# Grouping the small matrix products of a windowed-attention kernel by pairs of steps

## The chip, the cores and the metric

The kernel runs on one core of a Trainium2 chip. The metric is the device time of one launch, in microseconds (us). Three runs of the kernel before gave 4153.67, 4155.52 and 4155.97 us; the median is 4155.52 us.

## What is computed

Eight images `x` of 256 channels and 64 x 64 pixels go through two layers, each of which adds to its input. Both normalise over groups of 8 channels first (`_gn`).

Layer 0 makes a 3 x 3 filter for every pixel from two hidden maps and applies it to a third map:

```python
x1 = _conv1x1(x, w1, b1); x2 = _conv1x1(x, w2, b2); x3 = _conv1x1(x, w3, b3)
h = jnp.concatenate([x1, x2u], axis=1)            # x2u: 3 x 3 neighbours of x2
h = jax.nn.relu(_bn(h, ...)); h = _conv1x1(h, cw1)
h = jax.nn.relu(_bn(h, ...)); w = _conv1x1(h, cw2, cb2)
out = jnp.einsum('bgskhw,bgkhw->bgshw', x3u, w)   # 9 taps per pixel
```

Layer 1 adds an attention over 7 x 7 neighbours with 4 heads to a depthwise convolution whose nine results are weighted by a softmax:

```python
att = jax.nn.softmax(jnp.einsum('bdn,bdkn->bnk', q, uk + upe[None]), axis=-1)
out_att = jnp.einsum('bnk,bdkn->bdn', att, uv)
wts = jax.nn.softmax(jnp.einsum('oc,bchw->bohw', Wfc, x)..., axis=2)
hid = jax.nn.relu(_dwconv(xr, w1)); oc = _dwconv(hid, w2)
out_conv = jnp.sum(oc * wts, axis=1)
return rate1 * out_att + rate2 * out_conv
```

All is computed in fp32.

## The kernel before

An image is cut into 8 bands of 8 rows. Layer 1 takes the 64 bands in turn (`g` from 0 to 63). A band has 8 steps, s0 to s7: two channel halves `ct` by four column pairs `m`. Layer 0 of a later band runs inside the same steps (its maps 12 bands ahead, its hidden maps 11, its taps 10), so that layer 0 ends after about band 52. Before band 0 layer 0 runs alone.

The order on every engine is written out by hand. In `conv_layers_kernel` each step calls its parts in turn. `advance()` moves a clock by one, six times a step, and `after(n, f)` puts a piece of work n such places later. Each engine works through its instructions in that order.

A step does this:

- `scores` makes the attention scores of two 8 x 8 pixel tiles (L703, 64 x 64 parts of the array), and `weighted_values` (L747, 64 columns of the array) multiplies older probabilities with the values. Both write the tile `sco`, of two PSUM banks, of which there is one. DVE adds the mask and takes the maximum (L712), and `add_values` (L757) adds the weighted values to the output rows `xr`.
- `exponentials` (L720) and `probabilities` (DVE reciprocal L727, ACT scaling L729) finish the softmax. `transposed` (L735) turns the probabilities of the step before; ACT copies them (L737).
- `branch_weights` (L825) makes two of the nine weight maps of the dynamic convolution by 128 x 512 products, and ACT takes their exponential into `ex` (L830), of which there are three buffers. POOL adds them up (L1026).
- The depthwise convolutions are taps on DVE (L782, L808), four a step. Queries, keys, values and their transposes come at fixed steps (L637, L658, L563, L607).

At the end of a channel half `dynamic_sum` closes the weights: POOL makes the total (L838), DVE adds one and takes the reciprocal of the first half (L845, L846), then of the second half (L850), and POOL multiplies twice and adds to `xr` (L855, L856, L857). For `ct` 1 this falls into s0 to s2 of the next band, for `ct` 0 into s4 to s6.

Layer 0 inside the steps: `small_maps` (L328) in s0 with ACT's copies (L343, L347), `value_maps` (L369), `hidden_maps` (L418, L429) in two parts, and `tap_weights` (L447) in s1, s3 and s5, three taps each. Each tap is one DVE product (L460, two `prod` buffers) and one POOL addition to `xg` (L468). For the three taps of a call, DVE's products come 1, 2 and 7 (or 5) places later.

[...]two for `sco`, one for `acc` and five that the tag `gen` hands round.

Of the kernel before, what the change touches and what calls it, by code (L numbers as in the profile page):

```python
# [39 lines left out]
TG = 3  # L40
# [25 lines left out]
TAPS_AT = (1, 3, 5), (0, 2, 4)  # L66
PRODUCTS_AT = ((1, 2, 7), (1, 2, 5), (1, 2, 7)), ((7, 14, 10), (9, 17, 13), (12, 20, 16))
# [19 lines left out]
def conv_layers_kernel(ctx: ExitStack, tc: tile.TileContext, ins: dict, out: bass.AP):  # L87
# [98 lines left out]
    def layer1_loads():  # L186


        last = w1.tile([P, NCT, 1, C], F32, tag="rec", name="last", bufs=1)
        for f in late:  # L190
            f()
        nc.scalar.dma_start(out=last, in_=wfc_in[:, :, KK - 1 :])

        def first():
            nc.vector.tensor_scalar(wv, wv, rate1, None, ALU.mult)

        def difference(kt):
            nc.vector.tensor_sub(wfc[:, kt], wfc[:, kt], last[:, kt].to_broadcast([P, KK - 1, C]))  # L200

        return [first, lambda: difference(0), lambda: difference(1)]
# [22 lines left out]
    def gn_affine(sts, means, name, done):  # L225


        n = len(sts)
        mv = stat.tile([P, n, 2], F32, name=f"mv_{name}", tag=f"mv{n}")
        for ct, st in enumerate(sts):  # L230
            nc.vector.bn_aggr(mv[:, ct, :], st)
        mean, var = mv[:, :, 0], mv[:, :, 1]
        gm, d, sc, bi = (stat.tile([P, n], F32, name=f"{v}_{name}", tag=f"{v}{n}") for v in ("gm", "d", "sc", "bi"))

        def group_means(v, k):
            pg = ps.tile([P, n], F32, name=f"pg_{name}_{k}", tag="gen", bufs=5)
            nc.tensor.matmul(pg, means, v, start=True, stop=True)
            return pg


        def a1():
            pg = group_means(mean, 0)
            after(2, lambda: a2(pg))

        def a2(pg):
            nc.vector.tensor_copy(gm, pg)
            for ct in range(n):
                c = slice(ct, ct + 1)
                nc.vector.tensor_scalar(d[:, c], pg[:, c], mean[:, c], None, ALU.subtract)
                nc.vector.tensor_scalar(d[:, c], d[:, c], d[:, c], var[:, c], ALU.mult, ALU.add)  # L250
            after(5, a3)

        def a3():
            pg = group_means(d, 1)
            after(2, lambda: a4(pg))

        def a4(pg):
            nc.vector.tensor_scalar(sc, pg, GN_EPS, None, ALU.add)
            after(2, a5)

        def a5():
            nc.scalar.activation(sc, sc, AF.Sqrt)
            after(4, a6)

        def a6():
            nc.vector.reciprocal(sc, sc)
            for ct in range(n):
                c = slice(ct, ct + 1)
                nc.vector.tensor_scalar(bi[:, c], gm[:, c], sc[:, c], -1.0, ALU.mult, ALU.mult)
            done(sc, bi)  # L270

        after(3, a1)
# [15 lines left out]
    def scaled_weights(b):  # L288
# [11 lines left out]
        def through(bi):  # L300
            pb = ps.tile([P, 1 + NCT], F32, tag="gen", name=f"pb_{b}", bufs=5)
            for m, to, w in ((0, 0, w12), (0, 64, w12), (1, 0, w3[:, :, :P]), (2, 0, w3[:, :, P:])):
                for kt in range(NCT):
                    nc.tensor.matmul(
                        pb[to : to + w.shape[2], m : m + 1], w[:, kt], bi[:, kt : kt + 1],
                        start=(kt == 0), stop=(kt == NCT - 1),
                    )
            after(2, lambda: biases(pb))
# [11 lines left out]
    def small_maps(b, i):  # L320


        im = images[b]

        p12 = ps.tile([P, R // 2, W], F32, tag="gen", name=f"p12_{b}_{i}", bufs=5)
        for kt in range(NCT):
            for u in range(2):
                nc.tensor.matmul(  # L328
                    p12[64 * u : 64 * u + 64], im.w12s[:, kt, :],
                    im.xc[i][:, kt, u * BAND // 2 : (u + 1) * BAND // 2],  # L330
                    start=(kt == 0), stop=(kt == NCT - 1),
                )
        return lambda: write_maps(b, i, p12)
# [28 lines left out]
    def value_maps(b, i, mt):  # L362
# [4 lines left out]
        p3 = ps.tile([P, BAND], F32, tag="gen", name=f"p3_{b}_{i}_{mt}", bufs=5)  # L367
# [41 lines left out]
    def hidden_maps(b, i, at):  # L409
# [5 lines left out]
        def hidden(t):  # L415
            n = P if t == 0 else 96
            hid = w0.tile([P, R, W], F32, tag="hid", name=f"hid_{b}_{i}_{t}", bufs=2)
            nc.scalar.activation(  # L418
                hid[:n], im.x2[i][:n, t : t + R, :], AF.Relu, bias=bn1b[:n, t : t + 1], scale=bn1s[:n, t : t + 1]
            )  # L420
            hids.append(hid)

        def conv(first, last):
            if first == 0:
                im.ph = ps.tile([P, SR, W], F32, tag="gen", name=f"ph_{b}_{i}", bufs=5)
            for t in range(first, last):
                n = P if t == 0 else 96
                for q in range(NQR):
                    nc.tensor.matmul(  # L429
                        im.ph[q * REL : (q + 1) * REL], c1[:n, t], hids[t][:n, q * SR : (q + 1) * SR],  # L430
                        start=(t == 0), stop=(t == 2),
                    )

        def relu():
            nc.scalar.activation(h2n[i % 2][:, :, :W], im.ph, AF.Relu, bias=bn2b, scale=bn2s)

        hidden(0)
        for n, f in zip(at, (lambda: hidden(1), lambda: conv(0, 2), lambda: hidden(2), lambda: conv(2, 3), relu)):
            after(n, f)

    def tap_weights(b, i, u, alone, at):
# [3 lines left out]
        pw = ps.tile([P, TG, SR * HP], F32, tag="gen", name=f"pw_{b}_{i}_{u}", bufs=5)  # L445
        for j in range(TG):
            nc.tensor.matmul(  # L447
                pw[:, j], c2[:, TG * u + j], h2n[i % 2].rearrange("p r c -> p (r c)"), start=True, stop=True
            )

        def product(j):
            k = TG * u + j
            if alone and j == TG - 1:
# [11 lines left out]
            if alone and j == TG - 1:  # L465
# [11 lines left out]
        def gather(prod):  # L477
            if u == 0:
                im.part = score_tile(f"sum_{b}_{i}").rearrange("p t (s r c) -> p t s r c", r=SR, c=W)
            for t in range(2):  # L480
                nc.tensor.matmul(
                    im.part[:, t], ident, rows(prod)[:, t * SHARE // 2 : (t + 1) * SHARE // 2],
                    start=(u == 0), stop=(u == KK // TG - 1),
# [18 lines left out]
        for j, n in enumerate(at):  # L502
            after(n, lambda j=j: product(j))


    def norm_rows(b):
# [9 lines left out]
        def by_channel(both):  # L516
            pg = ps.tile([P, NCT, 2], F32, tag="gen", name=f"pgc_{b}", bufs=5)
# [33 lines left out]
    def values(b, j, ct):  # L551
# [3 lines left out]
        pv = ps.tile([P, R, W], F32, tag="gen", name=f"pv_{b}_{j}_{ct}", bufs=5)  # L555
# [45 lines left out]
    def value_tile(b, j, u):  # L601
        im = images[b]
        n = min(R, WP - j * R) * KW
        pvt = ps.tile([CHUNK, 2, C], F32, tag="gen", name=f"pvt_{b}_{j}_{u}", bufs=5)
# [22 lines left out]
    def queries(b, i, ct):  # L627
# [7 lines left out]
        pq = ps.tile([P, R, W], F32, tag="gen", name=f"pq_{nm}", bufs=5)  # L635
# [10 lines left out]
    def keys(b, i, ct):  # L646
# [7 lines left out]
        for a in range(first, last, R):  # L654
            n = min(R, last - a)
            pk = ps.tile([P, R, W], F32, tag="gen", name=f"pk_{b}_{i}_{ct}_{a}", bufs=5)
# [37 lines left out]
    def scores(b, i, ct, m, sco):  # L694
# [4 lines left out]
        nm = f"{b}_{i}_{ct}_{m}"  # L699
        for t in range(2):  # L700
            for h in range(2):
                c0 = (2 * m + t) * TQ
                nc.tensor.matmul(  # L703
                    sco[half[t], h, :NKEY], qb[half[h], 2 * m + t].rearrange("p r c -> p (r c)"),
                    kb[half[h], :, c0 : c0 + KW], start=True, stop=True,
                )

# [3 lines left out]
        for h in range(2):  # L711
            nc.vector.tensor_tensor_reduce(  # L712
                prob[:, h, :NKEY], sco[:, h, :NKEY], mask, -1.0, 3.0e38, ALU.add, ALU.min, nmax[:, h : h + 1]
# [17 lines left out]
    def transposed(nm, prob):  # L731
        ptp = ps.tile([CHUNK, 2, 2, P], F32, tag="gen", name=f"ptp_{nm}", bufs=5)
# [7 lines left out]
    def weighted_values(b, i, ct, m, pt, sco):  # L740
        im = images[b]
        po = sco[:, 0, 256 : 256 + 2 * NQ].rearrange("p (r c) -> p r c", r=R)
# [10 lines left out]
        return po  # L753

# [66 lines left out]
    def branch_weights(b, i, ct, m, j, ex):  # L821

        pf = ps.tile([P, R, W], F32, tag="gen", name=f"pf_{b}_{i}_{ct}_{m}_{j}", bufs=5)
# [8 lines left out]
    def dynamic_sum(b, i, ct, ex, oc):  # L832
# [6 lines left out]
        rec = w1.tile([P, BAND], F32, tag="rec", name=f"rec_{b}_{i}_{ct}", bufs=1)  # L839
# [29 lines left out]
    def beside(g, s):  # L869
# [52 lines left out]
        if 0 <= g + AHEAD < B * NB:  # L922
            bq_, iq = divmod(g + AHEAD, NB)
            if alone and s == 0:
                mid.append(lambda: small_maps(bq_, iq)())
# [4 lines left out]
        if 0 <= g + AHEAD - 1 < B * NB and s == (2 if alone else 1):  # L930
            at = (3, 7, 8, 12, 16) if alone else (5, 13, 14, 19, 21)
            end.append(lambda: hidden_maps(*divmod(g + AHEAD - 1, NB), at))
        if 0 <= g + AHEAD - 2 < B * NB and s in TAPS_AT[alone]:
            u = TAPS_AT[alone].index(s)
# [28 lines left out]
    with tc.manual_schedule():  # L963
# [20 lines left out]
        pending, before, conv = [], None, None  # L984
        for g in range(-AHEAD, B * NB):
            b, i = divmod(g, NB)
            for s in range(STEPS):
# [3 lines left out]
                if g >= 0:  # L991
                    if s == 0 and g + AHEAD < B * NB:
                        mid.append(small_maps(*divmod(g + AHEAD, NB)))
                    nm = f"{b}_{i}_{ct}_{m}"
                    sco = score_tile(nm)
                    weighted = [(a, weighted_values(*a, pt, sco)) for a, pt in pending]
                    prob, nmax = scores(b, i, ct, m, sco)
                    for a, po in weighted:
                        add_values(*a, po)
                    pending = [] if before is None else [(before[:-1], transposed(nm, before[-1]))]  # L1000
                    tot = exponentials(nm, prob, nmax)
                advance()
                if g >= 0:
                    ex, exb = w1.tile([P, 2, BAND], F32, tag="ex", name=f"ex_{nm}", bufs=3), ex if m else None
                    branch_weights(b, i, ct, m, 0, ex)
                    if m in (0, 2):
# [33 lines left out]
        for last in (before, None):  # L1040
            sco = score_tile(f"end{last is None}")
            weighted = [(a, weighted_values(*a, pt, sco)) for a, pt in pending]
            for a, po in weighted:
# [86 lines left out]
```

## Time and profile before

| | |
|---|---|
| median of three runs | 4155.52 us |
| profiled execution | 4152.64 us |
| its span | 4150.9 us |
| PE busy | 4022.6 us, 97% |
| DVE busy | 3591.9 us, 87% |
| ACT busy | 3081.0 us, 74% |
| POOL busy | 2923.0 us, 70% |
| granted TensorE clock | 0.993 |
| first scores of band 0 | 246.3 us |
| most bands with layer 0 beside them | 61.6 us |
| bands 57 to 61, without layer 0 | 53.1 us |

A busy share is an average over the whole span. Matmuls are pipelined and their ends are modelled, so PE's start times say more than its busy time. A band's time is read from one band's first score matmul to the next one's.

### The profile page before, as it was taken

Reading aid. Unit: us, or ns where it says so; the run is one execution under the profiler, and the core shown is the slowest. Engines: PE = TensorE matmul, PEld = TensorE weight load, DVE = VectorE, ACT = ScalarE, POOL = GpSimd, SP = SyncE. Lnnn points to the kernel's source line nnn. Section 1 sums busy time; section 2 is a strip of 40 time slices with the busy share of each in tenths; the row PEclk is TensorE's granted clock in tenths of the full one; section 3 lists DMA queues with packets and bytes.
Section 4 is the critical chain, followed back from the end, with each engine's and each line's share of the span. In section 5 each row is a group of like instructions: output and inputs, shape, how many; then the busy total and the mean of one; then the engine's idle time right before and its main releaser. Section 6 shows DMA issues by size and latency. Waiting matters only on the chain.

```text
span 4150.9 us, 72735 instructions
## 1 busy us (share of the span) xinstructions
PE 4022.6 (97%) x25292; PEld 2126.8 (51%) x25292; DVE 3591.9 (87%) x7248; ACT 3081.0 (74%) x7726; POOL 2923.0 (70%) x1902
## 2 busy tenths in 40 slices
PE   6789999999999999999999999999999999999998
PEld 3345555555555555555555555555555555455554
DVE  5878998899898898889998898888988889977777
ACT  3467778777787777877778777777778777687776
POOL 4767777677786777777777777777777677744554
PEclk8999999999999999999999999999999999999999
DMA  8854234234244233334234234244233233111100
GB/s 226 194 135 111 73 91 109 72 94 109 62 101 107 76 94 98 81 94 109 72 85 118 72 94 105 66 101 106 71 82 99 65 87 85 33 41 39 39 28 21
DMA packets 381264, 367.89 MB, mean 89 GB/s; under 512 B 55648, under 2 KB 282720, under 8 KB 380640
## 3 DMA queue, kind: packets, MB, share of 16 engines
q1 hardware_dynamic: 377568, 358.68, 34.3%
q8 instruction: 200, 3.28, 0.3%
q10 hardware_dynamic: 3328, 4.55, 0.3%
q14 instruction: 168, 1.38, 0.1%
HBM read 261.42 MB, written 101.71 MB: 87 GB/s over the span
## 4 chain that ended last, share of the span: by engine, by line
PE 71%; DVE 14%; POOL 6%; ACT 5%; DMA 2%; issue 2%; SPq 1%; POOLq 0%; ACTq 0%; DVEq 0%
PE pf L825 33%; PE ptp L735 5%; PE sco L747 5%; PE pk L658 5%; PE sco L703 5%; PE p L369 5%; DVE prod L460 4%; PE pq L637 4%; POOL xg L468 3%; PE pvt L607 2%; PE pv L563 2%; DVE acc L808 2%; PE pw L447 2%; DVE acc L782 2%; POOL ex L1026 2%
## 5 line engine op out<-in xcount | busy, mean ns | idle before, releaser
L825 PE MATMUL pf<-yp,c_wfc 128*128 128x512 f32 x4096 | 1930.5, 595 | 10.6 <-ACT vc L581 5.0
L468 POOL TENSOR_TENSOR xg<-xg,prod 128x1024 f32<-128x1024 f32 x549 | 1203.9, 2193 | 96.6 <-DVE prod L460 64.1
L825 PEld LDWEIGHTS pf<-yp,c_wfc 128*128 128x128 f32 x4096 | 729.9, 190 | 690.5 <-issue 619.4
L1026 POOL TENSOR_TENSOR ex<-ex,ex 128x1024 f32<-128x1024 f32 x384 | 907.7, 2364 | 61.9 <-ACT ex L830 57.2
L830 ACT ACTIVATE ex<-pf 128x512 f32<-128x512 f32 x1024 | 607.3, 593 | 297.9 <-POOL ex L1026 141.3
L782 DVE SCALAR_TENSOR_TENSOR acc<-yp,c_chan,acc 128x504 f32<-128x504 f32 (+3 forms) x1104 | 766.2, 694 | 42.3 <-ACT acc L773 21.7
L460 DVE SCALAR_TENSOR_TENSOR prod<-pw,c_par,x3q 128x1040 f32<-128x1040 f32 x576 | 733.9, 1281 | 66.8 <-PE pw L447 21.6
L808 DVE SCALAR_TENSOR_TENSOR acc<-hid,c_chan,acc 128x504 f32<-128x504 f32 (+3 forms) x1024 | 757.8, 740 | 20.2 <-ACT acc L802 2.1
L855 POOL TENSOR_TENSOR ex<-ex,rec 128x512 f32<-128x512 f32 x127 | 162.3, 1278 | 809.5 <-DVE rec L850 767.1
L729 ACT ACTIVATE prob<-prob,tot 128x196 f32<-128x196 f32 x1024 | 411.6, 450 | 387.2 <-DVE tot L727 386.4
L712 DVE CUSTOM_DVE_ANT_0 prob<-sco,c_mask 128x196 f32<-128x196 f32 x1024 | 325.5, 355 | 272.4 <-PE sco L703 272.0
L720 ACT ACTIVATE prob<-prob,nmax 128x196 f32<-128x196 f32 x1024 | 461.4, 454 | 46.9 <-DVE nmax L712 45.3
L747 PEld LDWEIGHTS sco<-pt,vt 112*64 112x64 f32 x8160 | 283.8, 137 | 182.3 <-issue 51.7
L737 ACT COPY pt<-ptp 112x512 f32<-112x512 f32 x511 | 297.0, 581 | 105.0 <-PE ptp L735 103.0
L735 PE MATMUL ptp<-ident,prob 128*112 128x128 f32 x2044 | 341.7, 287 | 31.2 <-ACT prob L729 30.5
L747 PE MATMUL sco<-pt,vt 112*64 112x64 f32 x8160 | 347.0, 227 | 0.0
L735 PEld LDWEIGHTS ptp<-ident,prob 128*112 128x112 f32 x2044 | 203.9, 133 | 201.4 <-issue 77.7
L703 PE MATMUL sco<-kb,qb 64*64 64x196 f32 x4096 | 295.2, 357 | 0.0
L563 PE MATMUL pv<-yp,c_wv 128*128 128x512 f32 (+2 forms) x576 | 247.3, 554 | 0.6
L369 PE MATMUL p<-xc,w3s 128*128 128x512 f32 x512 | 244.4, 601 | 0.0
L658 PE MATMUL pk<-yp,c_wk 128*128 128x512 f32 (+2 forms) x576 | 240.8, 545 | 0.0
L637 PE MATMUL pq<-yp,c_wq 128*128 128x512 f32 x512 | 240.6, 592 | 0.0
(140 smaller groups left out, 5294.0 us busy)
## 6 DMA issues: line engine op xcount, KB each, us to landing
x<-x3n SPq DMA_DIRECT2D x128, 264.0 KB, 2.1
x3q<-x SPq DMA_DIRECT2D x128, 264.0 KB, 7.2
xc<-in_x SPq DMA_DIRECT2D x64, 512.0 KB, 5.0
xg<-in_x SPq DMA_DIRECT2D x256, 128.0 KB, 4.8
x<-xg SPq DMA_DIRECT2D x256, 128.0 KB, 2.4
yp<-x SPq DMA_DIRECT2D x128, 256.0 KB, 3.3
xr<-x SPq DMA_DIRECT2D x64, 512.0 KB, 5.8
out_x<-xr SPq DMA_DIRECT2D x64, 512.0 KB, 3.1
```

The source lines that it names most:

```text
L369: nc.tensor.matmul(p3, im.w3s[:, kt, mt * P : (mt + 1) * P], im.xc[i][:, kt, :], start=(kt == 0), stop=(kt == NCT - 1),)
L460: nc.vector.scalar_tensor_tensor(prod[:, :, :RUN], pw[:, j, :RUN].unsqueeze(1).to_broadcast([P, SHARE, RUN]), par[:, PCB2 + k : PCB2 + k + 1],
L468: nc.gpsimd.tensor_add(im.xg[i], im.xg[i], rows(prod))
L703: nc.tensor.matmul(sco[half[t], h, :NKEY], qb[half[h], 2 * m + t].rearrange("p r c -> p (r c)"), kb[half[h], :, c0 : c0 + KW], start=True, ...
L720: nc.scalar.activation(prob[:, h, :NKEY], prob[:, h, :NKEY], AF.Exp, bias=nmax[:, h : h + 1], scale=-1.0, accum_out=tot[:, h : h + 1],)
L735: nc.tensor.transpose(ptp[:, h, ch], prob[:, h, ch * CHUNK : (ch + 1) * CHUNK], ident)
L747: nc.tensor.matmul(po[half[h], :, t * TQ : (t + 1) * TQ], im.vt[i + ch, m][:n, t, (2 * ct + h) * HD : (2 * ct + h + 1) * HD], pt[:n, h, ch ...
L782: nc.vector.scalar_tensor_tensor(o, yp[:, ct, ra + dr : rb + dr, ca + dc : cb + dc], chan[:, ct, CW1 + k : CW1 + k + 1], o, ALU.mult, ALU.add,
L808: nc.vector.scalar_tensor_tensor(o, hid[:, ra + dr : rb + dr, ca + dc : cb + dc], chan[:, ct, CW2 + k : CW2 + k + 1], o, ALU.mult, ALU.add,)
L825: nc.tensor.matmul(pf, wfc[:, kt, 2 * m + j, ct * P : (ct + 1) * P], images[b].yp[i][:, kt, PAD : PAD + R], start=(kt == 0), stop=(kt == N ...
L830: nc.scalar.activation(ex[:, j].rearrange("p (r c) -> p r c", r=R), pf, AF.Exp)
L1026: after(4, lambda ex=ex, exb=exb: nc.gpsimd.tensor_add(ex, ex, exb))
```

## The change

Even steps now do the small products for two steps. One `sco` tile takes the scores of both, side by side. A new tile, `small`, of one bank, takes the weighted values of two older steps, and, in s0, the small maps, and in s6 the hidden convolution, which is now done in one piece. `gen` has four banks. The mask and maximum stay one step at a time (`masked`). The odd steps' transposes stand after the first weight map instead of among the small products. Weighted values of s7 and s3 are added to `xr` in s2 and s6, where they were added in s1 and s5.

Taps are made two at a time in s1 to s5 (the last call has one); both products come at the first two places after. The buffer `rec` is gone (the reciprocal is written into `ex`), and `hid` has three buffers.

```diff
-TG = 3
+TG = 2, 3
...
-TAPS_AT = (1, 3, 5), (0, 2, 4)
-PRODUCTS_AT = ((1, 2, 7), (1, 2, 5), (1, 2, 7)), ((7, 14, 10), (9, 17, 13), (12, 20, 16))
+TAPS_AT = (1, 2, 3, 4, 5), (0, 2, 4)
+PRODUCTS_AT = ((1, 2),) * 5, ((7, 14, 10), (9, 17, 13), (12, 20, 16))
...
-        p12 = ps.tile([P, R // 2, W], F32, tag="gen", name=f"p12_{b}_{i}", bufs=5)
+        p12 = home[:, 2 * P :].rearrange("p (r c) -> p r c", r=R // 2)
...
-        def conv(first, last):
-            if first == 0:
-                im.ph = ps.tile([P, SR, W], F32, tag="gen", name=f"ph_{b}_{i}", bufs=5)
-            for t in range(first, last):
+        def conv(home):
+            ph = home[:, 2 * P : 3 * P].rearrange("p (r c) -> p r c", r=SR)
+            for t in range(3):
...
+    def score_of(sco, h, m):
+        return sco[:, h, m % 2 * NKEY : (m % 2 + 1) * NKEY]
...
+    def small_tile(nm):
+
+        return ps.tile([P, 4 * P], F32, tag="small", name=f"small_{nm}")
+
+    def weigh_steps(steps, home):
+
+        po = home[:, : 2 * P].rearrange("p (s r c) -> p s r c", s=2, r=R)
+        return [(a, weighted_values(*a, pt, po)) for a, pt in steps]
...
-        rec = w1.tile([P, BAND], F32, tag="rec", name=f"rec_{b}_{i}_{ct}", bufs=1)
+        rec = ex[:, 0]
...
-                    if s == 0 and g + AHEAD < B * NB:
-                        mid.append(small_maps(*divmod(g + AHEAD, NB)))
                     nm = f"{b}_{i}_{ct}_{m}"
-                    sco = score_tile(nm)
-                    weighted = [(a, weighted_values(*a, pt, sco)) for a, pt in pending]
-                    prob, nmax = scores(b, i, ct, m, sco)
+                    weighted = []
+                    if m % 2 == 0:
+                        sco = score_tile(nm)
+                        for e in range(2):
+                            scores(b, i, ct, m + e, sco)
+                        small = small_tile(nm)
+                        weighted, pending = weigh_steps(pending, small), []
+                        if s == 0 and g + AHEAD < B * NB:
+                            mid.append(small_maps(*divmod(g + AHEAD, NB), small))
+                        if s == 6 and convs:
+                            convs.pop()(small)
+                        if before is not None:
+                            pending.append((before[:-1], transposed(nm, before[-1])))
+                    prob, nmax = masked(nm, m, sco)
                     for a, po in weighted:
                         add_values(*a, po)
-                    pending = [] if before is None else [(before[:-1], transposed(nm, before[-1]))]
                     tot = exponentials(nm, prob, nmax)
                 advance()
                 if g >= 0:
...
                     branch_weights(b, i, ct, m, 0, ex)
+                    if m % 2:
+                        pending.append((before[:-1], transposed(nm, before[-1])))
```

## The prediction

> **What bounds the kernel now.** I read the page's busy shares first, then the start times of PE in one ordinary band (band 12, 1003.35 to 1064.93 us), then the timelines of POOL, DVE and ACT in it, since a busy PE need not be what sets the pace.
>
> ```profile
> PE 4022.6 (97%) x25292; PEld 2126.8 (51%) x25292; DVE 3591.9 (87%) x7248; ACT 3081.0 (74%) x7726; POOL 2923.0 (70%) x1902
> ```
>
> PE looks like the bound. Its timeline around step s5 (start, duration):
>
> ```profile
> 1038.00 1.88 PE L825 MATMUL pf<-yp,c_wfc 128*128 128x512 f32 x4
> 1039.81 0.42 PE L429 MATMUL ph<-hid,c_c 96*32 96x128 f32 x8
> 1040.17 0.69 PE L747 MATMUL sco<-pt,vt 112*64 112x64 f32 x16
> 1040.78 0.57 PE L703 MATMUL sco<-kb,qb 64*64 64x196 f32 x8
> 1041.28 0.65 PE L735 MATMUL ptp<-ident,prob 128*112 128x128 f32 x4
> 1041.77 1.88 PE L825 MATMUL pf<-yp,c_wfc 128*128 128x512 f32 x4
> 1043.49 1.88 PE L563 MATMUL pv<-yp,c_wv 128*128 128x512 f32 x4
> ```
>
> Starts are what counts: a 512-wide product holds PE for 1.72 us before another of its kind, and 1.81 us before a product on part of the array, so that entering costs 0.09 us. Weighted values, scores and transposes then take 0.61, 0.50 and 0.49 us. Adding up the undisturbed start-to-start times of a whole ordinary band gives 60.4 us. It takes 61.6, so 1.2 us are stalls, and they lie in s6 and s7. The other engines say why. POOL, then DVE, then ACT:
>
> ```profile
> 1019.00 1.28 POOL L855 TENSOR_TENSOR ex<-ex,rec 128x512 f32<-128x512 f32 x1 [6.12 <-DVE rec L850]
> 1020.36 1.27 POOL L856 TENSOR_TENSOR oc<-oc,ex 128x512 f32<-128x512 f32 x1
> 1021.71 1.28 POOL L857 TENSOR_TENSOR xr<-xr,oc 128x512 f32<-128x512 f32 x1
> 1022.94 4.46 POOL L468 TENSOR_TENSOR xg<-xg,prod 128x1024 f32<-128x1024 f32 x2
> ...
> 1034.62 4.45 POOL L468 TENSOR_TENSOR xg<-xg,prod 128x1024 f32<-128x1024 f32 x2
> 1039.03 2.37 POOL L1026 TENSOR_TENSOR ex<-ex,ex 128x1024 f32<-128x1024 f32 x1
> 1041.47 1.27 POOL L838 TENSOR_TENSOR ex<-ex 128x512 f32<-128x512 f32 x1
> 1042.70 2.17 POOL L468 TENSOR_TENSOR xg<-xg,prod 128x1024 f32<-128x1024 f32 x1
> ```
>
> ```profile
> 1042.78 2.38 DVE L845 TENSOR_SCALAR ex<-ex 128x512 f32<-128x512 f32 x1 [0.43 <-POOL ex L838]
> 1045.19 1.75 DVE L846 RECIPROCAL rec<-ex 128x256 f32<-128x256 f32 x1
> 1046.86 1.45 DVE L782 SCALAR_TENSOR_TENSOR acc<-yp,c_chan,acc 128x504 f32<-128x504 f32 x2
> ...
> 1049.79 1.75 DVE L850 RECIPROCAL rec<-ex 128x256 f32<-128x256 f32 x1
> ```
>
> ```profile
> 1048.41 0.81 ACT L729 ACTIVATE prob<-prob,tot 128x196 f32<-128x196 f32 x2 [3.71 <-DVE tot L727]
> ```
>
> From the end of L850 at 1018.92 POOL never rests until the total L838 ends at 1042.74, 23.8 us later. DVE waits for it, and L850 of the other channel half ends at 1051.54, 8.8 us on. I call these 32.6 us **half A**. ACT's scaling of the probabilities waited 3.71 us behind it, and PE's transposes behind that. From there DVE, ACT and PE lead back to the next L850 (1080.50): 29.0 us, **half B**. A and B close a loop of 61.6 us through all four engines. POOL's part of half A is 23.3 to 23.9 us in seven of an image's eight bands, and still 23.8 in bands 51 to 53, where PE has less to do. So PE's work is 1.2 us short of the bound, and a saving on PE is worth only what this loop passes on.
>
> [...]the 0.09 us above, 0.10 us more at L747 to L703 (152 ns between starts against 52), 0.06 us at L703 to L735, and some 0.05 us twice for a first weight load that nothing covers. [...]L845 takes 0.42 us (median) with POOL idle and 2.38 us above, where POOL's addition had just begun. [...]I let the mask of an even step wait for the scores of both steps; the trace of before has no such pair.
>
> **The change part by part.**
>
> *PE.* Per pair of steps before: 2 x (0.09 + 0.61 + 0.50 + 0.49) = 3.38 us. After, scores of two steps take [...]0.96 us; weighted values [...]1.09; even transposes 0.49; odd ones, now among full products, 0.44 (what L607 takes); entry 0.09: 3.07 us. The order scores, then weighted values, isn't in the trace; by its other switches the saving is 0.25 to 0.40, I take 0.31. Four pairs: 1.25 us. The hidden convolution in one piece, about 0.80 us against 0.58 + 0.36: 0.14 us. So PE's band falls from 60.4 to 59.0 us, and from 53.1 to 51.9 where layer 0 is over.
>
> *Tap weights in twos.* PE, DVE and POOL do the same nine; each bank is held for less, which pays for the fifth `gen` bank, as do the maps moved to `small`. But the order moves. POOL's queue before L838 held five additions since L850; products now come two in each of s2 to s5, so it holds six: +2.15 us. L845 then meets the next addition as before (2.38 us). And between DVE's first and second half reciprocal now stands a product: +1.21. Half A: 32.6 + 2.15 + 1.21 = 36.0 us. DVE gets there earlier: the wait described next 4.16, six more products 7.3, three masks 1.7, two pairs of additions 1.1, three steps of taps 9.0, keys 1.1, together 24.3 us. So POOL is the limit. ACT's exponentials also wait for these POOL additions through the three `ex` buffers, as before.
>
> *Weighted values a step later.* Those of s3 and s7 are added to `xr` by DVE in s6 and s2, now behind POOL's addition L857 to the same rows, a wait that no L757 has in the kernel before. POOL ends it 4.16 us after DVE starts past L850 (three operations, 1019.00 to 1022.99). DVE has a product (1.12) and the mask (0.56) before it, so it stands 2.4 us; queued behind it are the taps and the reciprocal that ACT's scaling waits for, then PE's odd transposes.
>
> *Half B*, on DVE alone: up to the end of that wait 4.16 us (a product and the mask of s6 lie in it), three more masks 1.7, two pairs of additions to `xr` 1.06, taps and small reciprocals of four steps 11.9, statistics 1.19 + 1.18, keys 1.11, L845 and L846 2.12, L850 1.66: 26.1 us. That is the floor. On the way that sets it before: the reciprocal of s6 comes at 6.2 us; ACT's scaling and the query copy, in its queue, end at 7.7, when PE's transposes get their bank; transposes, three big products and the values' transposes end at 12.2; then PE's group of s0 (scores 0.96, weighted values 1.09, small maps 0.87, transposes 0.49) ends at 15.7; ACT's copy and exponentials 17.2; weight exponential and scaling 18.9; a copy, eight map copies of 0.48, two more and the exponentials of s1 at 25.3; DVE's reciprocal, taps and L850: 28.5. I take 28.3.
>
> *The odd mask* no longer waits for PE (272.0 us in all before, mostly DVE idle that cost nothing). `rec` in `ex` and the third `hid` cost nothing: `ex` is held until L856 anyway.
>
> *Sum.* Loop 36.0 + 28.3 = 64.3 us against 61.6: +2.7. The first band of an image (68.8 us) has 3.2 us of POOL slack in its half A, where I take +1; mean +2.5. Layer 0 runs beside 53 bands: +133 us. Eleven bands without it, bound by PE, gain 1.2 each: -13. The 246 us before band 0 keep three taps a call: 0, within 5. Together +120 on the profiled execution's 4152.6 (span 4150.9 and 1.7 around it): 4273. That execution lies 2.9 under the median of the runs, so 4275.
>
> **The rivals.**
>
> *PE sets the pace and gets its saving.* For it: 97% busy. Against: half A doesn't move with PE's load. It needs one thing: that DVE doesn't stand at `xr`. Without those 2.4 us half B's floor is 23.7 and the loop can be 59.7; it decides once B is under 25.6 (61.6 - 36.0). Then bands take 59.7 to 60.4: 53 x -1.2 to -1.9, and -13: 4040 to 4080; 4000 if every stall goes.
>
> *DVE's floor.* ACT and PE keep up, B is 26.1, the loop 62.1: +0.5 x 53 - 13 = +14, 4170.
>
> *The banks.* Four `gen` banks, with ACT behind in s0 and s1 (7.84 us busy of 7.97 in s1): a further 0.7 us a band, 4310.
>
> *The switch isn't cheaper:* [...]PE at 60.4; the loop hides it, but the last bands lose their gain: 4288.
>
> **How the numbers follow.** Loop as summed, with banks and switch cases, 4220 to 4320: 0.56. DVE's floor and between, 4165 to 4220: 0.21. Faster: 0.18. Within 0.2% (8 us, about what a measurement of this kernel can't tell from none): 0.05. The range 4150 to 4320 leaves out the faster cases and a little above. Half B's bounds, 26.1 and 29.0 as before, give 4160 and 4312.
>
> **What would show it.** Right: POOL's way from the second half reciprocal to the total 26.0 us, half A 36; DVE's first addition to `xr` in s2 and s6 waiting for POOL, some 2 us each; ordinary bands 63 to 65 us, the last ones 52; PE's share down to about 94%. Wrong: half A under 34, or no such wait and bands under 61 us.

## The result, and the profile after

The changed kernel takes 4320.47 us (median of four runs, 4320.17 to 4323.61) against 4154.6 us before: a ratio of 1.0403, 95% interval 1.039 to 1.0415. The forecast was 4275 with a range up to 4320, so the direction is right and the size is not: +166 us where +120 was worked out.

The busy shares of the profiled execution (PE is TensorE, PEld its weight loads, DVE VectorE, ACT ScalarE, POOL GpSimd):

```profile
PE 4028.6 (93%) x25292; PEld 2174.3 (50%) x25292; DVE 3590.8 (83%) x7248; ACT 3075.5 (71%) x7726; POOL 2914.3 (67%) x1902
```

The same work is spread over 168 us more. The timeline of PE in s6 of band 10 (start, duration):

```profile
953.01 0.92 PE L701 MATMUL sco<-kb,qb 64*64 64x196 f32 x16
953.86 1.15 PE L750 MATMUL small<-pt,vt 112*64 112x64 f32 x32
954.94 0.87 PE L428 MATMUL small<-hid,c_c 128*32 128x128 f32 x24
957.68 0.78 PE L738 MATMUL ptp<-ident,prob 128*112 128x128 f32 x4 [1.88 <-ACT prob L732]
959.35 3.54 PE L837 MATMUL pf<-yp,c_wfc 128*128 128x512 f32 x4 [0.89 <-ACT vc L580]
962.69 2.06 PE L636 MATMUL pq<-yp,c_wq 128*128 128x512 f32 x4
```

The pair's scores take 0.85 us from start to start (forecast 0.96), its weighted values 1.08 (1.09): PE gets its saving. Both forecasts were estimates: the trace of before shows 0.06 to 0.10 us more between PE's starts at a switch between parts of the array, and not the reason. But PE then stands 1.88 us before the transposes and 0.89 more for a bank, and the four instructions of the 512-wide product that follows take 3.34 us to the next start instead of 1.72. POOL's timeline in the same band:

```profile
927.03 1.27 POOL L869 TENSOR_TENSOR xr<-xr,oc 128x512 f32<-128x512 f32 x1
928.26 4.44 POOL L467 TENSOR_TENSOR xg<-xg,prod 128x1024 f32<-128x1024 f32 x2
...
935.47 4.43 POOL L467 TENSOR_TENSOR xg<-xg,prod 128x1024 f32<-128x1024 f32 x2
939.86 2.38 POOL L1055 TENSOR_TENSOR ex<-ex,ex 128x1024 f32<-128x1024 f32 x1
942.19 4.45 POOL L467 TENSOR_TENSOR xg<-xg,prod 128x1024 f32<-128x1024 f32 x2
946.59 2.36 POOL L1055 TENSOR_TENSOR ex<-ex,ex 128x1024 f32<-128x1024 f32 x1
949.03 1.27 POOL L850 TENSOR_TENSOR ex<-ex 128x512 f32<-128x512 f32 x1
```

DVE's timeline from the total on:

```profile
950.34 2.39 DVE L857 TENSOR_SCALAR ex<-ex 128x512 f32<-128x512 f32 x1 [1.12 <-POOL ex L850]
952.76 1.75 DVE L858 RECIPROCAL ex<-ex 128x256 f32<-128x256 f32 x1
954.43 1.20 DVE L459 SCALAR_TENSOR_TENSOR prod<-pw,c_par,x3q 128x1040 f32<-128x1040 f32 x1
...
956.98 0.16 DVE L730 RECIPROCAL tot<-tot 128x2 f32<-128x2 f32 x1
...
958.55 1.75 DVE L862 RECIPROCAL ex<-ex 128x256 f32<-128x256 f32 x1
...
964.38 0.61 DVE L769 SCALAR_TENSOR_TENSOR xr<-small,bv,xr 128x128 f32<-128x128 f32 x2 [2.40 <-POOL xr L869]
...
966.34 0.16 DVE L730 RECIPROCAL tot<-tot 128x2 f32<-128x2 f32 x1
```

ACT's timeline there:

```profile
957.17 0.81 ACT L732 ACTIVATE prob<-prob,tot 128x196 f32<-128x196 f32 x2 [6.26 <-DVE tot L730]
```

Six additions to `xg` stand between the last multiplication (L869, which follows the second half reciprocal) and the total, where there were five. A tap product (954.43) stands between DVE's two half reciprocals. Both are as forecast. ACT's scaling waits 6.26 us (3.71 before) and is released by the small reciprocal at 956.98, before half A ends (960.30); PE's stop hangs on that one. From 957.68 to the next band's scores at 972.86 PE then has no further stop but the one of 0.89 us.

The groups of the waits on DVE's small reciprocal and at `xr`, over the whole run:

```profile
L732 ACT ACTIVATE prob<-prob,tot 128x196 f32<-128x196 f32 x1024 | 413.0, 452 | 643.1 <-DVE tot L730 643.1
L769 DVE SCALAR_TENSOR_TENSOR xr<-small,bv,xr 128x128 f32<-128x128 f32 x509 | 155.1, 347 | 332.7 <-POOL xr L869 275.6
```

The windows of 3 us of the same band: length, busy time of PE, its weight loads, DVE, ACT and POOL, then PE's granted clock as a share of full speed, and DMA:

```profile
956.00:959.00 3.00, 0.78 (x4) 0.37 (x4) 2.93 (x6) 1.76 (x5) 2.94 (x2) 1.00 0.00 0
959.00:962.00 3.00, 2.65 (x4) 1.14 (x5) 2.98 (x6) 2.75 (x8) 1.54 (x2) 0.60 0.00 0
962.00:965.00 3.00, 3.00 (x7) 1.27 (x6) 0.62 (x3) 1.32 (x5) 2.92 (x3) 0.83 0.00 0
```

After the stop the clock is halved: the clock records have it at 0.5 of full speed from 959.63 to 963.04 us. They hold 167 us at half clock in bands 0 to 52, in 33 stretches of 3.41 us and 8 of 6.83 us; before the change they hold 8 us. What sets the clock back is not shown; what is shown is that of PE's 41 stops of 1.84 to 2.53 us in these bands, 38 have a stretch that starts within 2.5 us of their end. The prediction did not use the clock.

### The profile page after: what moved, and what is told of

Same layout as the page of the kernel before. It is cut to its first block, busy times and chain, and to the rows that moved or that the text cites. A ratio compares the mean times of both kernels' runs of the same rounds, so it can differ in the third digit from the quotient of the medians.

```text
span 4318.5 us, 72795 instructions
## 1 busy us (share of the span) xinstructions
PE 4028.6 (93%) x25292; PEld 2174.3 (50%) x25292; DVE 3590.8 (83%) x7248; ACT 3075.5 (71%) x7726; POOL 2914.3 (67%) x1902
## 3 DMA queue, kind: packets, MB, share of 16 engines
q1 hardware_dynamic: 377568, 358.68, 33.4%
## 4 chain that ended last, share of the span: by engine, by line
PE 38%; DVE 23%; POOL 22%; issue 7%; ACT 7%; DMA 2%; SPq 1%; POOLq 0%; DVEq 0%; ACTq 0%
PE pf L837 19%; POOL xg L467 9%; DVE prod L459 5%; POOL ex L1055 5%; DVE acc L820 5%; PE pk L657 3%; DVE ex L857 3%; PE pq L636 2%; PE small L750 2%; DVE ex L858 2%; PE p L369 2%; DVE acc L794 2%; PE ptp L738 2%; POOL ex L867 2%; POOL oc L868 2%
## 5 line engine op out<-in xcount | busy, mean ns | idle before, releaser
L837 PE MATMUL pf<-yp,c_wfc 128*128 128x512 f32 x4096 | 1988.9, 610 | 62.0 <-ACT vc L580 29.8
L837 PEld LDWEIGHTS pf<-yp,c_wfc 128*128 128x128 f32 x4096 | 742.4, 194 | 802.5 <-issue 638.7
L867 POOL TENSOR_TENSOR ex<-ex 128x512 f32<-128x512 f32 x127 | 162.3, 1278 | 538.3 <-DVE ex L862 516.9
L769 DVE SCALAR_TENSOR_TENSOR xr<-small,bv,xr 128x128 f32<-128x128 f32 x509 | 155.1, 347 | 332.7 <-POOL xr L869 275.6
L738 PE MATMUL ptp<-ident,prob 128*112 128x128 f32 x2044 | 329.5, 283 | 94.1 <-ACT prob L732 77.8
L738 PEld LDWEIGHTS ptp<-ident,prob 128*112 128x112 f32 x2044 | 226.5, 135 | 289.8 <-issue 101.6
L740 ACT COPY pt<-ptp 112x512 f32<-112x512 f32 x511 | 294.0, 575 | 32.1 <-PE ptp L738 31.9
L750 PEld LDWEIGHTS small<-pt,vt 112*64 112x64 f32 x8144 | 264.0, 140 | 76.0 <-issue 76.0
L750 PE MATMUL small<-pt,vt 112*64 112x64 f32 x8144 | 299.6, 228 | 0.0
L636 PE MATMUL pq<-yp,c_wq 128*128 128x512 f32 x512 | 254.7, 621 | 12.5 <-ACT ex L842 11.9
L446 PEld LDWEIGHTS pw<-h2n,c_c 128*128 128x128 f32 x1152 | 174.1, 192 | 164.2 <-issue 103.5
```

The lines of the kernel that those rows point to most:

```text
L636: nc.tensor.matmul(pq, wq[:, kt, ct * P : (ct + 1) * P], im.yp[i][:, kt, PAD : PAD + R], start=(kt == 0), stop=(kt == NCT - 1),)
L738: nc.tensor.transpose(ptp[:, h, ch], prob[:, h, ch * CHUNK : (ch + 1) * CHUNK], ident)
L750: nc.tensor.matmul(po[half[h], :, t * TQ : (t + 1) * TQ], im.vt[i + ch, m][:n, t, (2 * ct + h) * HD : (2 * ct + h + 1) * HD], pt[:n, h, ch ...
L837: nc.tensor.matmul(pf, wfc[:, kt, 2 * m + j, ct * P : (ct + 1) * P], images[b].yp[i][:, kt, PAD : PAD + R], start=(kt == 0), stop=(kt == N ...
```

## The experiments

All times are medians beside runs of the kernel before on the same chip. Half A and half B are those of the prediction, read in the second and third band of an image; "half clock" is the time at half clock in bands 0 to 52.

| kernel | us | ratio, interval | half A | half B | band | half clock |
|---|---|---|---|---|---|---|
| before | 4154.6 | | 32.6 | 29.0 | 61.6 | 8 |
| after | 4320.5 | 1.0403 (1.0390, 1.0415) | 36.1 | 28.8 | 64.9 | 167 |
| e1 after, taps by three | 4396.5 | 1.0576 (1.0545, 1.0607) | 33.1 | 33.6 | 66.6 | 212 |
| e2 before, taps by two | 4384.0 | 1.0546 (1.0515, 1.0577) | 36.1 | 29.9 | 66.0 | 236 |
| e3 after, later additions | 4436.7 | 1.0673 (1.0598, 1.0747) | 36.0 | 31.7 | 67.8 | 317 |
| e4 e1 and e3 together | 4233.9 | 1.0185 (1.0155, 1.0214) | 32.6 | 31.0 | 63.6 | 99 |
| e5 after, unread products | 4352.4 | 1.0484 (1.0454, 1.0515) | 36.1 | 28.5 | 64.6 | 17 |
| e6 by three, later in s2, s6 | 4156.0 | 1.0006 (0.9995, 1.0016) | 32.8 | 28.9 | 61.6 | 21 |
| e7 moved, later in s2, s6 | 4121.6 | 0.9927 (0.9905, 0.9950) | 32.5 | 28.9 | 61.4 | 14 |
| e8 before, four banks | 4239.5 | 1.0213 (1.0183, 1.0242) | 33.4 | 29.5 | 62.8 | 17 |
| e9 after, later in s2, s6 | 4305.0 | 1.0357 (1.0327, 1.0387) | 36.1 | 28.8 | 64.9 | 167 |
| e10 e9, unread products | 4316.8 | 1.0385 (1.0355, 1.0415) | 36.1 | 27.1 | 63.2 | 51 |
| e11 before, taps moved | 4125.5 | 0.9925 (0.9896, 0.9954) | 31.8 | 29.0 | 60.8 | 11 |
| e12 after, taps moved | 4369.0 | 1.0511 (1.0480, 1.0541) | 33.0 | 33.4 | 66.4 | 191 |
| e13 e5 in five bands of eight | 4304.8 | 1.0359 (1.0329, 1.0389) | 36.1 | 28.5 | 64.5 | 14 |
| e14 e10 in five bands of eight | 4248.0 | 1.0222 (1.0192, 1.0252) | 36.1 | 27.1 | 63.2 | 51 |

The theory was the loop of the prediction; the rivals were the banks (four `gen` banks and a late ACT) and PE's own pace. The 174 us of half clock that the expectations give for the kernel after count 6.83 us in band 53 too.

### e1: taps by three again

```diff
-TG = 2, 3
+TG = 3, 3
-TAPS_AT = (1, 2, 3, 4, 5), (0, 2, 4)
-PRODUCTS_AT = ((1, 2),) * 5, ...
+TAPS_AT = (1, 3, 5), (0, 2, 4)
+PRODUCTS_AT = ((1, 2, 7), (1, 2, 5), (1, 2, 7)), ...
```

> The kernel after with the tap weights again three at a time at the old places (s1, s3, s5, with products 1, 2 and 7 or 5 places later); the small products stay by pairs of steps. Loop theory (half A grew by a sixth POOL addition and one DVE product, half B is half A's counterpart and hardly shrank): half A goes back to 32.6 us, half B is 29 to 30 because DVE still stands at xr, an ordinary band takes 62 to 63 us, the time is about 4190 (4165 to 4230). Banks theory (four gen banks and ACT late set the pace): bands stay at about 65 us, or get longer since three-tap calls hold a bank longer, time 4310 or more. If PE sets the pace: under 4110.

Half A went back by 3 us, as expected, and half B grew by 4.8 us, which nothing of mine expected. PE's timeline of e1 in s6 and s7:

```profile
973.90 0.60 PE L606 MATMUL pvt<-ident,vc 128*112 128x128 f32 x4
978.49 2.50 PE L837 MATMUL pf<-yp,c_wfc 128*128 128x512 f32 x4 [3.99 <-ACT qb L640]
```

DVE's timeline of the same kernel there:

```profile
973.69 0.61 DVE L769 SCALAR_TENSOR_TENSOR xr<-small,bv,xr 128x128 f32<-128x128 f32 x2 [2.41 <-POOL xr L869]
974.22 1.29 DVE L459 SCALAR_TENSOR_TENSOR prod<-pw,c_par,x3q 128x1040 f32<-128x1040 f32 x1
...
976.87 0.16 DVE L730 RECIPROCAL tot<-tot 128x2 f32<-128x2 f32 x1
```

PE stands 3.99 us for a bank, until ACT has copied the queries; ACT's copy stands behind the scaling, and that behind DVE's reciprocal of s6. DVE has its wait at `xr` and then the third tap product ahead of it. So here half B depends on what DVE does in s6 between the second half reciprocal (L862) and the small one (L730). The change had moved a product away from there and put the wait at `xr` in its place; e1 has both.

### e2: taps by two, in the kernel before

The tap part of the change alone, with five banks and the small products step by step.

> The kernel before with the tap weights two at a time at the new places, and nothing else of the change: small products step by step, five gen banks. Loop theory: half A 36.0 us (a sixth addition +2.15, one product +1.21), half B shorter by the product that left it, 27.5 to 29, a band 63.5 to 65 us, time 4250 to 4330. Banks theory: with five banks the bands stay at 61.6 us, time 4150 to 4165.

Half A is 36.1, as expected; half B did not get shorter, and the time lies above the 4250 to 4330 of the loop theory. This part alone costs 5.5%, more than the whole change. PE's timeline of e2 in s6:

```profile
974.93 1.10 PE L736 MATMUL ptp<-ident,prob 128*112 128x128 f32 x4 [3.49 <-ACT prob L730]
975.82 2.83 PE L826 MATMUL pf<-yp,c_wfc 128*128 128x512 f32 x4
```

PE stands 3.49 us, about what half A grew by, and half clock follows: the four instructions of the product take 2.67 us to the next start.

### e3 and e4: additions to `xr` later

```diff
-                        add_values(*a, po)
+                        after(4, lambda a=a, po=po: add_values(*a, po))
```

> The kernel after with one edit: DVE's additions of the weighted values to xr come four places later in the step, so DVE no longer stands behind POOL's addition to the same rows. Loop theory: the wait of some 2.2 us at these additions goes, half A stays 36 us, half B falls from 28.8 to 25.8 to 27, bands 62 to 63 us, time 4150 to 4210. Banks theory: half B is set by ACT and the gen banks, not by that wait, bands stay at about 65 us, time 4300 to 4320.

> Both edits together: taps three at a time as before, and DVE's additions to xr four places later. Loop theory: half A 32.6 us and half B 26 to 27.5 us, loop 59 to 60 us, so PE (59.0 us a band) and the loop are about level: bands 59.5 to 60.5 us, time 4030 to 4080, faster than before. Banks theory: bands at 64 us or more, time about 4300.

Both missed: half B is 31.7 and 31.0 us, where 25.8 to 27 and 26 to 27.5 were expected. Against the kernel after it grew by 2.9 us in e3; against e1 it fell by 2.6 in e4. The edit took the wait at POOL away and brought another one, in s0. DVE's timeline of e3 there:

```profile
945.68 0.61 DVE L769 SCALAR_TENSOR_TENSOR xr<-small,bv,xr 128x128 f32<-128x128 f32 x2 [3.00 <-PE pf L837]
```

ACT's timeline of e3 there:

```profile
943.72 1.43 ACT L343 ACTIVATE x<-small,bias 32x252 f32<-32x252 f32 x3
945.18 0.47 ACT L347 ACTIVATE x<-small,bias 32x256 f32<-32x256 f32 x1
945.67 0.60 ACT L842 ACTIVATE ex<-pf 128x512 f32<-128x512 f32 x1
```

The view names PE, whose product had long been done. DVE starts 0.03 us after ACT's last copy of the small maps, which lie in the same bank, and it does so in 51 bands of the run. The later addition now comes after these copies in program order, and, as this timing shows, waits for them, 3.00 us here, although both engines only read the bank. So the two runs don't tell the theories apart; e6 and e9 do, where s0 and s4 keep the old place.

### e5: products that keep PE busy

```diff
                         if s == 6 and convs:
                             convs.pop()(small)
+                            for _ in range(16):
+                                nc.tensor.matmul(small[:, 3 * P :], ident, ident, start=True, stop=True)
```

> The kernel after with 16 more products of 128 x 128 (1.75 us), which nobody reads, in each s6 between the hidden convolution and the transposes, where PE stands 1.9 to 2.5 us in about half of the bands. Clock theory (the stop itself is bound to come, but a stop of that length is followed by one or two stretches of 3.41 us at half clock, on the way through half B): the half-clock time in the bands falls from 174 us to under 90, and the time, although PE does more, falls by 20 to 60 us, to 4260 to 4300. If the half clock costs nothing, since the loop waits for POOL and DVE: 4320, or up to 4350 where the extra products stand in the way.

The products took 3.67 us, not the 1.75 that I wrote: each is two instructions of 0.115 us. Half clock in the bands fell to 17 us, and the five bands of an image that stop in s6 got shorter by 0.3 to 1.25 us although their transposes came later. The fourth, seventh and eighth, where PE has no such stop to fill, got 1.9 to 3.7 us longer, which turned the total. e13 repeats it without those.

### e6 and e7: additions later in s2 and s6 alone

```diff
-                        add_values(*a, po)
+                        after(4, lambda a=a, po=po: add_values(*a, po)) if m else add_values(*a, po)
```

e6 has this with taps by three, e7 with taps by two at other places:

```diff
-TAPS_AT = (1, 2, 3, 4, 5), (0, 2, 4)
-PRODUCTS_AT = ((1, 2),) * 5, ...
+TAPS_AT = (1, 3, 4, 5, 6), (0, 2, 4)
+PRODUCTS_AT = ((1, 2), (1, 2), (1, 1), (1, 2), (1, 2)), ...
```

> Taps three at a time, and DVE's additions to xr four places later in s2 and s6 alone; those of s0 and s4 at their old place. The last set showed that the later addition in s0 stood 3.0 us behind ACT's copies of the small maps, which read the same bank; here it does not. Loop theory: half A 32.6 us as measured there, the way from a band's start to the second half reciprocal goes back from 18.7 to 16.2, half B from 30.8 to 28.4, an ordinary band 60.9 us, time 4234 - 53 x 2.4 = 4105 (4080 to 4140), just under the kernel before. If the four banks hold PE up at s7 as they do with taps by three and early additions (4.0 us at one product a band): 4200 or more.

> The kernel after with two edits: tap weights two at a time in s1, s3, s4, s5, s6, so that only four of POOL's additions come between the second half reciprocal and the total, and DVE's additions to xr later in s2 and s6. Loop theory: POOL's part of half A falls from 26.1 to about 21.7 us and half A to about 31, half B 28, so that PE (59.0 us a band) sets the pace: bands 59 to 61 us, no long stops of PE and so no half clock, time 4010 to 4110. If the loop is not what holds the bands (banks, ACT): 4200 or more.

e6 is level with the kernel before: against e1, half B fell from 33.6 to 28.9. The hoped-for 4105 did not come, since half B is 28.9 and not 28.4 and half A 32.8 and not 32.6. PE still has short waits for banks there (32 us in 36 waits for the copy of the queries); that they hold half B up was not tested. e7 beats both kernels, by 0.7% and 4.6%, but misses the 4010 to 4110 that were expected. POOL's timeline of e7:

```profile
897.51 2.36 POOL L1055 TENSOR_TENSOR ex<-ex,ex 128x1024 f32<-128x1024 f32 x1
901.81 4.54 POOL L467 TENSOR_TENSOR xg<-xg,prod 128x1024 f32<-128x1024 f32 x2 [1.93 <-DVE prod L459]
```

With four additions POOL's part is 23.7 us, not the 21.7 expected: POOL now rests 1.93 us for DVE's product, so its own work no longer sets half A.

### e8: four banks, in the kernel before

Only the five of the tag `gen` became four.

> The kernel before with four gen banks in place of five, nothing else (taps by three, small maps and hidden convolution still in gen). Theory that the two taps a time belong to the four banks: a three-tap tile keeps a bank through the reciprocal, PE has no bank for the products of s6 and s7 and stands some 4 us a band, half A stays 32.6, half B grows from 29 to 33 or more: 4350 to 4480. Loop theory alone, in which banks do not matter: 4155 to 4175.

2.1% slower: 1.25 us in an ordinary band, 0.8 of it in half A, between the two expectations. So banks count, for less than the 4 us that I expected: without the wait at `xr` the reciprocal of s6 is not late. It ends 4.7 us after half A, as in the kernel before, and 7.4 us after it in e1.

### e9, e10, e13, e14: the wait at `xr` and the clock

e9 is the kernel after with the later additions of e6; e10 adds the unread products to it; e13 and e14 put the products only into bands 0, 1, 2, 4 and 5 of an image.

> The kernel after with DVE's additions to xr four places later in s2 and s6 alone. This is the wait which the prediction put at 2.4 us in half B, without the new wait in s0 that the first try at moving it brought. If that wait is on the path by its whole length: half B 28.8 - 2.4 = 26.4, half A 36.1, bands 62.5 us, time 4200. If PE's own work after its stop is what sets half B, and the wait lies beside it: half B 27.5 to 28.8, bands 63.6 to 65 us, 4260 to 4330, with more half-clock time than the 174 us of the kernel after, since DVE and ACT are ready sooner and PE is not.

> The same with the 16 unread products in s6, which kept the clock up. If half clock is what eats the gain of the later additions: no half-clock time in the bands that stop in s6, half B 26 to 27.5 there, under the run without the products by 0.5 us a band or more in these bands; bands in which PE does not stop there are longer by up to 3 us, as they were before. If the clock is a minor matter: half B within 0.3 us of the run without the products.

> The kernel after with the 16 unread products (1.75 us of PE) in s6 of the bands 0, 1, 2, 4 and 5 of each image alone. From the band lengths of the run with them everywhere: these five bands shorter by 1.25, 0.30, 0.31, 0.45 and 0.69 us, 3.0 us an image over 6.6 images, so 4320 - 20 = 4300 (4290 to 4310). If the clock has no part: 4320 or more.

> The same products in the same five bands, on the kernel with the later additions to xr in s2 and s6. If the wait at xr and the half clock hold half B side by side, each hiding the other: half B 27.1 us in these bands (28.9 with the later additions alone, 28.5 with the products alone), bands 63.2 us, 1.9 + 1.8 + 1.7 + 2.2 + 2.1 = 9.7 us an image over 6.6 images under the 4305 of the later additions alone: 4240 (4230 to 4255). If only one of them counts: 4285 to 4305.

In the ordinary bands, half B is 28.8 with the wait and half clock, 28.8 without the wait (e9), 28.5 without half clock (e13), and 27.1 with neither (e14). Neither is worth much alone, both together 1.7 us: they lie side by side. Runs without the products say the same. Bands 12, 20 and 36 of the kernel after have no half clock in half B, and it is 28.5 us there, as in e13. In e9 half B is 28.7 us in bands 20 and 36, with 2.2 us of half clock in it, and 30.2 in bands 12 and 28, with 5.3. e13 gives the share of the clock in the whole change, about 16 us; e14 is 57 us under e9. Both times lie within what was expected. More half clock was expected in e9, and did not come. PE's timeline in s6 of band 10 of e9:

```profile
958.46 0.78 PE L738 MATMUL ptp<-ident,prob 128*112 128x128 f32 x4 [2.60 <-ACT prob L732]
960.13 3.62 PE L837 MATMUL pf<-yp,c_wfc 128*128 128x512 f32 x4 [0.89 <-ACT vc L580]
963.59 1.88 PE L636 MATMUL pq<-yp,c_wq 128*128 128x512 f32 x4
```

The same of e14 (the products of 941.76 are the unread ones):

```profile
941.76 3.84 PE L1024 MATMUL small<-ident 128*128 128x128 f32 x32
945.43 0.60 PE L738 MATMUL ptp<-ident,prob 128*112 128x128 f32 x4
946.11 1.99 PE L837 MATMUL pf<-yp,c_wfc 128*128 128x512 f32 x4
947.93 1.88 PE L636 MATMUL pq<-yp,c_wq 128*128 128x512 f32 x4
```

The first weight map (L837) starts 51.4 us after the band's first scores in both; e14's later transposes take up the wait for a bank. From there to the queries (L636) it is 3.46 us against 1.82, and this 1.64 us is the half clock.

### e11 and e12: the taps moved, without the later additions

> The kernel before with tap weights two at a time in s1, s3, s4, s5, s6 (four POOL additions ahead of the total, as in the best version so far), and nothing else of the change. Loop theory: half A 32.5 us or less, half B about 29, so the order of the taps alone takes back what taps by two cost (half A 36.1): bands 61 to 61.8 us, time 4130 to 4165. If PE paces it (60.4 us a band and its stalls): 4130. If the two-at-a-time form itself costs, wherever it stands: 4250 or more.

> The kernel after with the taps moved to s1, s3, s4, s5, s6 and the additions to xr left where the change put them. Loop theory: half A 32.6 us (POOL's part 23.7), half B 29 to 31, since the wait at xr in s6 is still there and a product (1.2 us) again stands behind it ahead of the reciprocal that ACT's scaling waits for: bands 62 to 63.5 us, time 4160 to 4240. If the taps' place is all that matters: 4120, as with the later additions.

e11, the kernel before with nothing but taps by two in s1, s3, s4, s5, s6, is 0.75% faster: half A 31.8, no long stop of PE in an ordinary band, and 11 us of half clock where the kernel before has 8. That is what e7 has with all of the change in it, so the gain of e7 is not shown to come from the pairs of steps. The two are level in different ways: from band 53 on, where layer 0 is over, e7 takes 579 us and e11 596, but bands 0 to 52 take 3298 and 3280. What e7 has beyond the taps pays where layer 0 is over, and costs as much where it runs. e12 missed upwards: half A 33.0, but half B 33.4, as in e1. DVE's timeline of e12 in s6:

```profile
972.83 0.61 DVE L769 SCALAR_TENSOR_TENSOR xr<-small,bv,xr 128x128 f32<-128x128 f32 x2 [2.40 <-POOL xr L869]
973.36 1.29 DVE L459 SCALAR_TENSOR_TENSOR prod<-pw,c_par,x3q 128x1040 f32<-128x1040 f32 x1
...
976.01 0.16 DVE L730 RECIPROCAL tot<-tot 128x2 f32<-128x2 f32 x1
```

The reciprocal of s6 starts 7.3 us after half A's end, as in e1, against 6.0 in the kernel after: a product again stands between the wait at `xr` and it. In e7, with the additions later, it starts at 4.2 with the same product ahead of it. What comes on top is half clock: half B of e12 is 31.9 us in band 10, which has none, 33.4 in band 9 with one stretch and 34.9 in band 18 with two.

## Why the prediction was wrong in size

**Half A was right, in the ordinary bands.** 36.0 forecast, 36.1 measured; POOL's way 26.0 and 26.1. It is 36.0 to 36.1 in all eight kernels with taps by two in s1 to s5, and 31.8 to 33.4 in the others, whatever the small products and banks are: the order of the taps is shown to be its cause.

**PE's saving was right.** The last bands went from 53.1 to 51.8 us (51.9 forecast), the share of PE to 93% (94%). It was not passed on while layer 0 runs, as said. The rival in which the switch isn't cheaper would have left the last bands at 53.1.

**"I take 28.3" for half B was too low**, by 0.5 us: 28.8. This is the step that failed in the ordinary bands, and two things are in it. The working itself came to 28.5, and no reason stands for the 0.2 us less. And it priced every product of PE at full clock. Band 12 of the kernel after, which has no half clock, shows how good the way was otherwise. PE's timeline there, where half A ends at 1092.27 us:

```profile
1089.65 0.78 PE L738 MATMUL ptp<-ident,prob 128*112 128x128 f32 x4 [1.90 <-ACT prob L732]
1091.32 1.98 PE L837 MATMUL pf<-yp,c_wfc 128*128 128x512 f32 x4 [0.89 <-ACT vc L580]
1093.14 1.88 PE L636 MATMUL pq<-yp,c_wq 128*128 128x512 f32 x4
...
1099.94 0.65 PE L738 MATMUL ptp<-ident,prob 128*112 128x128 f32 x4 [1.05 <-ACT qb L640]
```

The reciprocal of s6 ends at 6.2 us (6.2 forecast), the transposes behind ACT's query copy start at 7.7 (7.7), the next band's scores at 12.2 (12.2), and half B is 28.5. In band 10 the same transposes start at 8.2 us, with no wait ahead of them: PE's own queue, partly at half clock, is now the longer way, and the wait at `xr` lies beside it. So the missing term is the half clock, 0.3 us of the 0.5.

The rival of DVE's floor, 26.1, is not reached even without that wait (27.1 in e14). The first rival needed half B under 25.6 without the wait: it falls, too.

**The first band of an image, "+1", is +3.5** (484.1 to 508.4 us over the seven up to band 48). This is the second step that failed: its 3.2 us of slack on POOL were no cover, and half A grew from 35.8 to 39.6 us. POOL's timeline of the kernel after in band 8, the first of an image:

```profile
803.79 4.46 POOL L467 TENSOR_TENSOR xg<-xg,prod 128x1024 f32<-128x1024 f32 x2 [1.88 <-DVE prod L459]
...
812.47 4.47 POOL L467 TENSOR_TENSOR xg<-xg,prod 128x1024 f32<-128x1024 f32 x2 [1.90 <-DVE prod L459]
816.89 2.37 POOL L1055 TENSOR_TENSOR ex<-ex,ex 128x1024 f32<-128x1024 f32 x1
819.33 1.27 POOL L850 TENSOR_TENSOR ex<-ex 128x512 f32<-128x512 f32 x1
```

POOL waits for DVE's products twice, and what follows the second wait is on the path. The products set half A here, and they came later. Four banks alone make this band 3.0 us longer (e8: 505.1 us over the seven), taps by two alone as much (e2: 505.4), with half A at 36.8 and 38.1; how the two share it in the kernel after was not separated.

**The sum again**, on the spans. First bands: 7 x 3.5 = 24 (7 in the forecast). The 46 other bands up to 52: 2822.4 to 2976.2, +154 or 3.3 each (2.7 each, 124). From band 53 on -7, not -13: band 53 still has a half A of 36 us and is 4 us longer. Before band 0 -3. Together 168 against 120. Of the 30 missing in the other bands, 14 are shown to be the clock's (e13: 2961.8), and the step from 28.5 to 28.3 is 0.2 a band, some 9. In the first bands, which are 17 over the forecast, no single cause was isolated.

**The banks** were given 0.7 us a band, which would make 4310. Near as that is to the result, the ordinary bands need no such term: at full clock half B is what the working has without it. In the kernel before four banks cost 1.25 (e8). In e1 the stop behind a late reciprocal in s6 is a wait for a bank; whether five banks would avoid it was not tested. With the additions where the change put them, taps by three (e1) are slower still; with later ones (e6) they are not. So the parts are no sum: taps by two cost 5.5% alone (e2), the rest 5.8% without them (e1), and both 4.0%.

## What to carry to other kernels

Where a loop runs through several engines, moving an instruction changes what stands ahead of the one that another engine waits for; count what lies between the release and that instruction on every queue, and put work that nobody waits for behind it. Here 38 of PE's 41 stops of 1.84 to 2.53 us in bands 0 to 52 of the kernel after had a stretch of 3.41 or 6.83 us at half clock that started within 2.5 us of their end, so a stop has to be priced with what follows. Before crediting a gain to the large part of a change, run the small part alone: here an order of taps gave as much as the best version with all of it.

## What the runs showed of the hardware

- In bands 0 to 52 of the kernel after half clock came in stretches of 3.41 us (33) and 6.83 us (8). Stops shorter than such a stretch could be enough: 1.88 and 0.89 us within 5 us in band 10 were followed by one stretch. In band 12 of the same run 1.90 and 0.89 us were followed by none, nor were the six stops of 1.76 or 1.77 us in the seventh bands of the images; in band 10 of e1 a stop of 3.99 us was followed by one. So the length of a stop alone does not decide; what else does was not tested.
- One 512-wide instruction, of the four that make a product, takes 0.85 us to the next start at half clock, against 0.43 at full clock (medians of L837 in the kernel after). At full clock its record lasts 0.59 us, so successive records overlap.
- In e3 DVE's addition from the bank of `small` stood 3.00 us and started 0.03 us after the last of ACT's eight copies from it, although both only read it.
